# Layers 0 and 3 of a four-layer image network: a new planner with two clocks orders the instructions, layer 0 leaves the waves in two halves, and its third tile is copied by ScalarE

## The chip, the cores and the metric

The kernel runs on one core of a Trainium2 chip. The metric is device time in microseconds (us) for one execution, from a handful of runs; the profile is one further execution under the hardware profiler. TensorE (PE) multiplies matrices into PSUM; VectorE (DVE), ScalarE (ACT) and GpSimd (POOL) do elementwise work; SyncE (SP) and GpSimd issue the transfers here. [...]

## The reference

The input x is float32, 4 images x 48 channels x 256 x 256. Four layers, each of the form x = x + f(groupnorm(x)):

```
layer 0:  h = w_in (48 -> 192) . x;  h = depthwise 3x3(h);  g = gelu(h1) * h2   (96 each)
          y = w_out (96 -> 48) . g;  y = irfft2(rfft2(y in 8x8 blocks) * fft_w)
layers 1, 2:  four scans (down, up, right, left): row = x_row + conv1d(previous row)
layer 3:  y = w_in (48 -> 288) . x;  y = irfft2(rfft2(y in 8x8 blocks) * fft_mask)
          y = depthwise 3x3(y);  g = gelu(y1) * y2   (144 each);  out = w_out (144 -> 48) . g
```

## The kernel before, in words

Everything is float32. The images are worked on in two pairs. Only layers 0 and 3 matter here; the scans between them have an order of their own.

**Layer 0** (`layer0`, L150) goes through 64 strips of 8 rows of an image pair. Per strip n:

- `fetch` (L228) loads 9 rows through SP; `normed` (L237) applies the group norm on ScalarE.
- `fill(n, True)` with `hidden_rest` (L269): two pieces, each two matmul calls (L272) for the third tile of hidden channels, `rest`, copied out of PSUM by VectorE (L276). `fill(n, False)` with `hidden`: two pieces for the other 128 channels (L264), copied into `main` by ScalarE (L267). `halo` (L249) lets GpSimd carry two rows over from the strip before (L256).
- The depthwise convolution of `main` is done on TensorE by two *lanes* (`lane`, L280): each takes half the channels and, for each of two images, does nine taps as matmuls with diagonal weights (L293). A *lane round* is one tap of each lane; lane 1 starts four rounds after lane 0. When its nine taps are done, lane 0 takes gelu on ScalarE (L304), lane 1 multiplies on VectorE (L307), which frees their PSUM tiles.
- The convolution of `rest` is done on VectorE by a *unit* (`unit`, L312): a first tap on ScalarE (L322), 16 half-tile taps on VectorE (L328), gelu on ScalarE (`curve`, L336 to L338), two products (L342).
- `mixed` (L355) multiplies by w_out (L363, L370), ScalarE copies to y (L376); `turned` (L382) transposes (L387, copies L391); `waves` (L396) goes to the 64 waves (L405), VectorE applies the mask (L409); `back` (L416) returns to pixels in two rounds of a loop (64 matmul calls each way of q0, L430), VectorE adds the residual (16 instructions, L441) and takes statistics (L448); GpSimd's queue stores (L451).

All PSUM tiles of layer 0 come from one pool of four (tag "w"): the two lanes hold one each, the pieces share the others.

**Layer 3** (`layer3`, L846) goes through 33 steps of 8 rows for each of two image pairs (the last is a short tail): `normed` (L945, ScalarE L950), `turned`, `waves`, eight pieces of `spectra` (two matmul groups L996 and two masks on VectorE each, L998 and L1002), five pieces of `back` (`pixels`: L1033, copies L1042) that fill the tiles a0, a1, b0, b1, m; lanes for a and m (L1054), for the lower half of b (L1070; `lower_gate` L1077: gelu L1080, product L1081), gates L1097 with gelu L1091; VectorE units for the upper half of b (first tap L1111, taps L1114, products L1125); `store` with `mixed` (L1132: L1140, L1150, residual L1163).

**What sets the order.** [...] `in_turns` (L516) runs rounds: it advances both lanes by one tap, adds to a credit, emits the next piece from `work` while the credit is not negative and the piece's condition holds (a piece is: condition, TensorE cost, what to emit, VectorE cost), and then lets `aside` (L549) emit taps of the units for as long as a running sum `ahead` (TensorE's time spent less the pieces' VectorE costs, between -4.0 and 2.5) is above 0. What follows a unit's taps (`curve`, the products) waits for a count of calls. In layer 0 `mixed` waits for all six users of a strip (`taken`) and then for four more askings (`gone`, L484). Neither knows of ScalarE.

## Time and profile before

| what | us |
|---|---|
| median of 3 runs (lowest, highest) | 13858.08 (13811.36, 13867.86) |
| the profiled execution's own time | 13799.8 |
| its span | 13798.0 |
| TensorE busy (90% of the span) | 12409.4 |
| VectorE busy (53%) | 7347.8 |
| ScalarE busy (28%) | 3850.6 |
| GpSimd busy (10%) | 1334.0 |

Stages by the first matmuls of each in the trace: statistics of the input to 251 us; layer 0 to about 3231; the two scan layers to about 9178; layer 3 to the end.

A line of a group reads: source line, engine, operation, tile written <- tiles read, shapes, count | total busy us, mean ns | idle time of the engine just before, and what ended it. A line of the waits: engine, tile, line <- what it waited for: us in total, times, longest. In a row of stretches the granted TensorE clock (1.00 is full speed) comes after the five engines' busy times, then the share of the DMA engines that was busy and GB/s. "Issue" means that the profile shows nothing that the engine waited for. Busy matmul time is modelled at its ends, so full is not peak.

### The profile page before, as it was taken

To read this page: it belongs to the slowest core of one execution; us is meant where nothing else is said; L and a number is where in the kernel's file an instruction comes from. 1 tells how busy PE (TensorE), PEld (TensorE's weight loads), DVE (VectorE), ACT (ScalarE), POOL (GpSimd) and SP (SyncE) were. 2 spreads that over 40 slices of the span, in tenths; PEclk is the share of its full clock that TensorE was granted. 3 is DMA by queue.
4 is the path that set the end of the run, shared out by engine and by line. 5 is a ranking of instruction groups with operands and counts; after the bars stand their busy time and mean duration, and the time that the engine had idled before them with its cause. 6 is when DMAs were issued, how large, how long until landed. Compare 5 with 4: busy or idle time off the path is not lost.

```text
span 13798.0 us, 419051 instructions
## 1 busy us (share of the span) xinstructions
PE 12409.4 (90%) x195140; PEld 7360.8 (53%) x195140; DVE 7347.8 (53%) x11937; ACT 3850.6 (28%) x4710; POOL 1334.0 (10%) x977
## 2 busy tenths in 40 slices
PE   2888898888999899879998998779999999999999
PEld 1333333335777677657776776544444445444444
DVE  6777777774333334443333344455555556555555
ACT  1333333332223100002232000034443434443443
POOL 0000010000000003430000014400000000000000
PEclk9999999999999999989999999889999999999999
DMA  7222222225755876767657767711101101101100
GB/s 169 53 50 52 56 54 53 50 54 96 153 142 152 159 153 143 190 156 152 134 153 169 149 133 183 183 37 26 26 22 26 26 22 26 26 22 26 26 22 24
DMA packets 1170329, 1224.15 MB, mean 89 GB/s; under 512 B 1027668, under 2 KB 1031756, under 8 KB 1107724
## 3 DMA queue, kind: packets, MB, share of 16 engines
q1 hardware_dynamic: 1070476, 649.55, 23.6%
q0 software_dynamic: 87488, 445.55, 11.7%
q10 hardware_dynamic: 10624, 102.24, 3.7%
q8 instruction: 1532, 25.10, 0.8%
q14 instruction: 209, 1.71, 0.0%
HBM read 699.76 MB, written 497.42 MB: 87 GB/s over the span
## 4 chain that ended last, share of the span: by engine, by line
PE 78%; DMA 7%; DVE 6%; ACT 4%; issue 3%; POOL 1%; SPq 1%; ACTq 0%; DVEq 0%; POOLq 0%
PE acc L632 35%; PE pd L1054 10%; PE pd L293 9%; PE pz L996 4%; PE pd L1070 4%; PE pp L1033 4%; DMA blk<-x 3%; PE po L1150 2%; PE ph L272 2%; ACT u L950 2%; PE ph L264 2%; DMA x<-blk 2%; DMA gx<-in_x 1%; DVE acc L328 1%; POOL blk L825 1%
## 5 line engine op out<-in xcount | busy, mean ns | idle before, releaser
L632 PE MATMUL acc<-line,w_down 96*96 96x256 f32 x12240 | 2650.7, 379 | 53.1 <-DMA in<-x 31.3
L632 PEld LDWEIGHTS acc<-line,w_down 96*96 96x96 f32 x12240 | 1996.1, 163 | 707.0 <-issue 53.8
L1054 PE MATMUL pd<-z_a,diag 32*32 32x512 f32 x37152 | 1853.0, 606 | 44.9 <-issue 31.5
L293 PE MATMUL pd<-main,diag 32*32 32x512 f32 x36864 | 1522.9, 653 | 112.3 <-issue 103.9
L632 PE MATMUL acc<-line,w_left 96*96 96x256 f32 x6120 | 1358.1, 385 | 248.7 <-DVE line L815 248.7
L1114 DVE SCALAR_TENSOR_TENSOR acc<-z_b,wd,acc 128x1024 f32<-128x1024 f32 (+1 forms) x1056 | 1328.9, 1260 | 311.5 <-ACT acc L1111 279.6
L632 PE MATMUL acc<-line,w_right 96*96 96x256 f32 x6120 | 1335.2, 380 | 102.5 <-DVE line L776 38.1
L632 PEld LDWEIGHTS acc<-line,w_left 96*96 96x96 f32 x6120 | 1014.2, 166 | 592.2 <-DVE line L815 254.7
L328 DVE SCALAR_TENSOR_TENSOR acc<-rest,wd,acc 128x1024 f32<-128x1024 f32 x1024 | 1279.0, 1299 | 2.0
L632 PEld LDWEIGHTS acc<-line,w_right 96*96 96x96 f32 x6120 | 1002.1, 164 | 435.6 <-DVE line L776 40.1
L1070 PE MATMUL pd<-z_b,diag 32*32 32x512 f32 x18432 | 1065.5, 603 | 34.0 <-DVE z L1002 22.3
L293 PEld LDWEIGHTS pd<-main,diag 32*32 32x32 f32 x36864 | 534.9, 107 | 917.0 <-issue 800.6
L776 DVE SCALAR_TENSOR_TENSOR line<-acc,b_right,in 96x256 f32<-96x256 f32 x1020 | 489.2, 480 | 879.6 <-PE acc L632 835.1
L998 DVE TENSOR_TENSOR z<-pz,mask 128x512 f32<-128x512 f32 x1024 | 702.8, 686 | 458.8 <-PE pz L996 455.0
L695 DVE TENSOR_TENSOR line<-acc,in 96x256 f32<-96x256 f32 x1020 | 429.3, 421 | 944.5 <-PE acc L632 928.4
L108 ACT ACTIVATE nrm<-nrm 96x4 f32<-96x4 f32 (+2 forms) x4 | 0.8, 204 | 3323.3 <-DVE nrm L107 3323.3
L1054 PEld LDWEIGHTS pd<-z_a,diag 32*32 32x32 f32 x37152 | 593.6, 103 | 587.0 <-issue 431.1
L735 DVE SCALAR_TENSOR_TENSOR line<-acc,b_down,in 96x256 f32<-96x256 f32 x992 | 476.0, 480 | 808.7 <-PE acc L632 808.7
L1033 PEld LDWEIGHTS pp<-c_inv,z 64*64 64x64 f32 x36864 | 602.1, 136 | 463.4 <-issue 253.2
L1033 PE MATMUL pp<-c_inv,z 64*64 64x64 f32 x36864 | 672.2, 222 | 170.6 <-DVE g_b L1081 86.0
L825 POOL TENSOR_TENSOR blk<-blk,line 96x1024 f32<-96x1024 f32 x248 | 705.7, 2873 | 860.2 <-DVE line L815 444.6
L815 DVE SCALAR_TENSOR_TENSOR line<-acc,b_left,in 96x256 f32<-96x256 f32 x992 | 475.5, 479 | 525.4 <-PE acc L632 525.4
(158 smaller groups left out, 12337.0 us busy)
## 6 DMA issues: line engine op xcount, KB each, us to landing
blk<-x ACTq DMA_DIRECT2D x64, 1536.0 KB, 23.2
in<-x SPq DMA_DIRECT2D x248, 384.0 KB, 11.5
dn<-line POOLq DMA_DIRECT2D x124, 768.0 KB, 9.6
rt<-line POOLq DMA_DIRECT2D x124, 768.0 KB, 10.2
in<-rt SPq DMA_DIRECT2D x124, 768.0 KB, 7.3
in<-dn SPq DMA_DIRECT2D x120, 768.0 KB, 7.1
in<-up SPq DMA_DIRECT2D x240, 384.0 KB, 11.0
up<-blk POOLq DMA_DIRECT2D x56, 1536.0 KB, 23.9
```

The lines of the kernel that those rows point to most:

```text
L293: nc.tensor.matmul(pd[32 * j : 32 * j + 32, i], diag[s, t, :], z[s, R2 * j + t // 3 : R2 * j + t // 3 + R2, t % 3 : t % 3 + W], start=(t = ...
L328: nc.vector.scalar_tensor_tensor(to, at(t, r), wd[:, 1, t : t + 1], to, ALU.mult, ALU.add)
L632: self.nc.tensor.matmul(acc, w[:, t, :], carry[:, :, t : t + m], start=(t == 0), stop=(t == 2))
L735: nc.vector.scalar_tensor_tensor(inner(line), acc, bd, new[p][r], ALU.add, ALU.add)
L776: nc.vector.scalar_tensor_tensor(blocks(inner(line)), blocks(acc), br, new, ALU.add, ALU.add)
L825: (nc.vector if w0 == 0 else nc.gpsimd).tensor_tensor(part, part, inner(ln[p][:, f::2])[..., lo:hi].rearrange("p w i h -> p i h w"), ALU.add)
L996: nc.tensor.matmul(pz[:, b, 0 : 2 * HD], xf[s, q, :], wi[s, :], start=True, stop=True)
L998: nc.vector.tensor_tensor(z[:, q, 0 : 2 * n].rearrange("p (b c) -> p b c", b=2), pz[:, :, 0:n], mask[:, :, 0:n].to_broadcast([128, 2, n]), ...
L1033: nc.tensor.matmul(pp[to, l, q1, :], z[f, q0 + q, k * NM + 64 * c : k * NM + 64 * c + 64], self.inv1[f, :], start=True, stop=True,)
L1054: nc.tensor.matmul(pd[32 * j : 32 * j + 32, i, 0:n, :], diag[s, 2 if g == "m" else half, t, :], zt[g][s, R2 * j + t // 3 : R2 * j + t // 3 ...
L1070: nc.tensor.matmul(pd[to, i], diag[s, half, t, :], zt[f"b{half}"][s, R2 * j + t // 3 : R2 * j + t // 3 + R2, t % 3 : t % 3 + W], start=(t ...
L1114: nc.vector.scalar_tensor_tensor(made[0], at(t), wd[:, half, t : t + 1], made[0], ALU.mult, ALU.add)
```

## The change

The diff, cut to what it does. `hidden_rest` copies with ScalarE, both chunks in one instruction where they are of equal height; `back` handles one half (q0 = 0 or 8) per call and each half is a piece of its own; the planner keeps two clocks, `self.pe` and `self.dve`. Taps are emitted while `self.dve` is at most `self.pe + 1.0`; a piece with a VectorE cost is emitted only when `self.dve < self.pe + 1.5`; what follows the taps has a due time on the TensorE clock; a tile counts as free, and a strip or step as ready for `mixed`, only when the TensorE clock has passed the VectorE clock of its last use (`until`). `gone` is removed. In layer 3 the same planner is used, with clock entries for the gates and products; its computation is untouched.

```diff
@@ hidden_rest
+                if all(r1 - r0 == R2 for r0, r1 in chunks):
+                    chunks, ph = [(chunks[0][0], chunks[-1][1])], ph.rearrange("p i r w -> p (i r) w").unsqueeze(1)
                 for i, (r0, r1) in enumerate(chunks):
-                    nc.vector.tensor_copy(rests[n % 2][:, 0, r0 + 1 : r1 + 1, 1 : W + 1], ph[:, i, 0 : r1 - r0, :])
+                    nc.scalar.copy(rests[n % 2][:, 0, r0 + 1 : r1 + 1, 1 : W + 1], ph[:, i, 0 : r1 - r0, :])
@@ lane of layer 0, after the product L307
+                            self.after(self.pe + 1.0, 1.3)
+                            until[n] = max(until.get(n, 0.0), self.dve)
@@ unit of layer 0
-                last = [(3, 0.0, curve)] + [
-                    (2 - k, 1.28, lambda k=k: product(slice(64 - 64 * k, 128 - 64 * k))) for k in range(2)
+                last = [(0.3, 0.0, curve)] + [
+                    (2.2 - k, 1.28, lambda k=k: product(slice(64 - 64 * k, 128 - 64 * k))) for k in range(2)
                 ]
-                return lambda: (n, 1) in ready, start, taps, last
+                return lambda: self.pe >= full.get(n, 1e9), start, taps, done, last
@@ back
-            def back(n, z):
+            def back(n, z, q0):
...
-                for b in range(2):
+                for b in range(2 if q0 == 0 else 0):
                     nc.sync.dma_start(res[64 * b : 64 * b + C], self.x0[p, b * C : (b + 1) * C, h0 : h0 + RB, :])
...
-                for q0 in range(0, NQ, 8):
+                for q0 in (q0,):
...
+                if q0 + 8 < NQ:
+                    return
@@ work of layer 0
+                                if rest:
+                                    full[n] = self.pe + 4.0
-                        yield always, 1.8, go, 1.2 * rest
+                        yield always, 1.8, go, 0.0
...
-                            lambda: taken.get(n - 1, 0) == 6 and gone(), 4.0, lambda: state.update(y=mixed(n - 1)),
+                            lambda: taken.get(n - 1, 0) == 6 and self.pe >= until[n - 1], 4.0,
+                            lambda: state.update(y=mixed(n - 1)), 0.0,
...
-                        yield always, 2.2, lambda: back(n - 1, state["z"]), 7.0
+                        yield always, 2.0, lambda: back(n - 1, state["z"], 0), 1.7
+                        yield always, 1.1, lambda: back(n - 1, state["z"], 8), 4.4
-            self.in_turns([lane(0), lane(1)], work(), 0.52, self.aside([unit(n) for n in range(len(strips))]))
+            self.in_turns([lane(0), lane(1)], work(), 0.54, [unit(n) for n in range(len(strips))])
@@ in_turns, new
+        self.pe, self.dve = 0.0, 0.0
+        side, going = self.aside(units), True
...
+            self.pe += 0.54 * moved
             credit = min(credit + pace * moved, 2.0)
+            while piece and (credit >= 0 or not moved) and piece[0]() and (not piece[3] or self.dve < self.pe + 1.5):
                 piece[2]()
+                if piece[3]:
+                    self.after(self.pe + 1.0, piece[3])
+                self.pe += piece[1]
+                credit, moved = max(credit - piece[1], -5.0), 1
                 piece = next(pieces, None)
+            got = True
+            while got:
+                got = next(side, None)
+                going = got is not None
+            idle = 0 if moved else idle + 1
+            self.pe += 0.0 if moved else 0.3
+    def after(self, when, cost):
+        self.dve = max(self.dve, when) + cost
@@ aside, new
+        def due():
+            while later and self.pe >= later[0][0]:
+                at, cost, work = later.pop(0)
                 if cost:
+                    self.dve = max(self.dve, at) + cost
                 work()
...
+                begun[k] = self.pe + 3.0
                 units[k][1]()
...
+                while k not in begun or self.dve > self.pe + 1.0 or self.pe < begun[k]:
+                    begin(k)
+                    due()
+                    yield False
...
+                self.dve = max(self.dve, begun[k]) + cost
@@ layer 3
+                self.after(self.pe + 1.0, 1.3)                      (lower_gate; gate: 0.1 + 0.6 * k)
+                until[step] = max(until.get(step, 0.0), self.dve)
...
-                last = [(3, 0.0, curve)] if half == 0 else [(2, 1.28, product)]
+                last = [(0.3, 0.0, curve)] if half == 0 else [(0.3, 1.28, product)]
...
-                    free = lambda: last not in steps or k == 4 or taken.get((last, order[k]), 0) == units[order[k]]
+                    free = lambda: last not in steps or k == 4 or (
+                        taken.get((last, order[k]), 0) == units[order[k]]
+                        and self.pe >= until.get((last, order[k]), 0.0)
+                    )
...
-                    done = lambda: step in full and all(taken.get((step, g), 0) == units[g] for g in order)
+                    done = lambda: step in full and self.pe >= until[step] and all(
+                        taken.get((step, g), 0) == units[g] for g in order
+                    )
```

## The prediction

> **What bounds the kernel now.** I read the busy table in the page's order first (TensorE 90% of the span, VectorE 53%, ScalarE 28%), then the granted clock by stage, then TensorE's waits and its timeline in the two stages that the change touches. Layer 0 runs from 251 to 3231 us, the two scan layers to about 9178 us, layer 3 to 13770 us. The scans use neither planner and keep their time.

> A row of the stretches below: from:to, length, then busy time (and instructions) of TensorE, its weight loads, VectorE, ScalarE, GpSimd; then granted clock, DMA share and GB/s. First line: the middle of layer 0. The others: two short pieces of single strips.

> ```profile
> 600.00:2990.00 2390.00, 2115.25 (x40933) 855.80 (x40933) 1775.62 (x2359) 883.17 (x823) 226.84 (x207) 0.93 0.24 53
> ```

> ```profile
> 1500.00:1505.00 5.00, 2.12 (x40) 1.07 (x38) 5.00 (x5) 1.84 (x2) 1.53 (x1) 0.91 0.00 0
> 1505.00:1510.00 5.00, 4.62 (x66) 2.43 (x72) 5.00 (x5) 2.78 (x3) 0.00 (x0) 0.50 0.00 0
> ...
> 1545.00:1550.00 5.00, 3.03 (x72) 1.35 (x40) 5.00 (x5) 2.15 (x2) 1.53 (x1) 1.00 0.00 0
> 1550.00:1555.00 5.00, 3.71 (x57) 1.87 (x72) 5.00 (x6) 2.44 (x3) 0.00 (x0) 0.69 0.00 0
> ```

> See two losses: TensorE is idle 11% of layer 0's middle, and its clock is 0.93 there, because a piece with little TensorE work is followed by one at 0.50 or 0.69. VectorE is full in just these pieces. TensorE's own waits in that stretch (total us, times, longest):

> ```profile
> PE pt L387 <- DVE g L307: 140.0, 49, 3.3
> PE pd L293 <- issue: 91.2, 52, 4.5
> PE po L430 <- issue: 21.7, 9, 4.6
> PE pt L387 <- ACT gl L304: 12.3, 25, 0.5
> ```

> and what VectorE does ahead of that product (start, length, from the timeline):

> ```profile
> 1544.87 1.29 DVE L276 COPY rest<-ph 128x512 f32<-128x512 f32 x2 [0.51 <-PE ph L272]
> ...
> 1546.08 4.03 DVE L328 SCALAR_TENSOR_TENSOR acc<-rest,wd,acc 128x1024 f32<-128x1024 f32 x3
> ...
> 1550.02 1.21 DVE L307 TENSOR_TENSOR g<-gl,pd 128x1024 f32<-128x1024 f32 x1
> ...
> 1551.29 1.19 PE L387 MATMUL pt<-c_ident,y 112*128 112x112 f32 x8 [3.26 <-DVE g L307]
> ```

> The four PSUM tiles are all in use: the second transpose tile takes the one that lane 1 has just finished, and its product (L307) stands behind two copies (L276) and three taps (L328). So once per strip TensorE stands 3.3 us and then runs at half clock. The other large wait, "issue", has no releaser: it comes while the strip's loads run (at 1527.70 and 1571.40 the DMA share is 0.5 to 0.9), so I take it to be late instructions.

> In layer 3 (9178 to 13770 us: clock 0.99, TensorE 4303.04 of 4592 us) the waits are small:

> ```profile
> PE pp L1033 <- DVE g_b L1081: 75.4, 59, 3.0
> PE pp L1033 <- issue: 49.6, 65, 2.9
> PE pz L996 <- DVE g_a L1097: 30.0, 27, 1.1
> ```

> [...]

> **One strip of layer 0 now.** The first mixed matmuls (L363) start at 302.67, those of the last strip at 3210.81: 63 periods of 46.16 us. TensorE's work at full clock, from start to start in the timeline: 18 lane rounds, two of them in 2.28 us (1540.57 to 1542.85), 20.5; main matmuls (L264) 2 x 1.92; rest matmuls (L272) 2 x 1.91; L363 1.92; L370 1.90; transposes 2 x 0.98; L405 1.67; L430 2.0: sum 37.6 us. The stretch of 2390 us holds 51.8 strips, so the waits are 140.0/51.8 = 2.7 us (L307), 112.9/51.8 = 2.2 (issue), all others 0.4: 5.3. The rest, 46.16 - 37.6 - 5.3 = 3.3, is slow clock (a mean of 0.93 costs 3.2).

> **The change part by part.**
> 1. *Rest copy to ScalarE.* Per strip VectorE loses 4 copies, 2.58 us (two take 1.29), ScalarE gains 2 of 1.01 us. ScalarE goes from 883.17/51.8 = 17.1 to 19.1 us per strip: hidden. VectorE falls from 34.3 (1775.62/51.8) to 31.7 us, below TensorE's 37.6, so it can't be the bound. The copies leave the queue ahead of L307: 1.29 us less in that wait. Behind the new copies on ScalarE stand the first tap L322 (which needs them anyway; its 290.5 us of waiting on VectorE ends), gelu L304 and the y copies; a wait for the rest matmuls (1.9 us) now holds those up. GpSimd's halo copy then waits for ScalarE instead, which nobody needs for 10 us.
> 2. *Two clocks.* Taps are emitted while the VectorE clock is at most 1.0 us ahead of TensorE's, so at a product at most 2.3 us is queued plus its own 1.2, against 1.29 + 3.94 + 1.2 now. Prices in the plan are near the measured (tap 1.28 against 1.22 to 1.30, gate 1.3 against 1.21, VectorE's halves of back 1.7 + 4.4 against 3.26 + 2.46 in sum). The transposes still come about one lane round after the product's emission, so the wait of 2.7 us falls to between 0.1 and 1.4; I take 0.5. Bounds 0 and 2.7.
> 3. *Clock.* Without a 3.3 us hole the half clock goes; the issue waits of up to 4.5 us still cause it at times. 3.3 falls to 0.6 (bounds 0.2 and 3.3).
> 4. *Mixed waits for the clock instead of four askings.* The gate's VectorE time must have passed: 2.3 to 3.6 us after the lane ends, against 3.1 now (1528.25 to 1531.39). Behind it stand all later pieces of the strip; the fill for the next strip comes some nine lane rounds later, and lane 0 needs it 14 rounds after the strip's end. Now there are two rounds to spare; one round later means TensorE can wait for ScalarE's main copy, up to 1.1 us. Other waits go from 0.4 to 0.8 (bounds 0.2 and 3).
> 5. *Back in two halves.* Same 128 matmul records and 16 additions; each half needs one PSUM tile, not two. The residual load is issued with the first half, the store and the four statistics with the second: SP's and GpSimd's queues keep their order. If the second half and mixed follow each other, mixed's second tile waits for 1.63 us of additions; in part 4's bound.
> 6. *Issue waits* stay at 2.2: the DMAs and the instruction count are unchanged.
> Sum: 37.6 + 0.5 + 2.2 + 0.8 + 0.6 = 41.7 us, 4.46 less, x 63 = **281 us**.
> 7. *Layer 3.* 64 full steps in 4592 us, near 71 us each with the two short ones; VectorE 2651.55/4592 = 58%. Its largest wait, L1081, is late because gelu L1080 stands on ScalarE behind the eight L950 (4.0 us at 11521.71), and the plan knows no ScalarE clock: it stays. L996 behind L1097 (30.0 us) and a part of the others goes, and the earlier taps cost nothing as VectorE is idle there. I take 0.5 us per step, 32 us; bounds -1.5 and +2 us per step (-96 and +128), as a reordered step can pair its lanes better or worse and nothing in the trace shows which.
> Total 281 + 32 = 313. The profiled execution took 13799.8 us (span 13798.0 and 1.8 around it): 13487 for it. The runs' median, 13858.08, is 58 higher; taken from that, **13545 us**.

> **Rivals.**
> A, the forecast, 0.50: 13545, its own range 13430 to 13680.
> B, the waits go altogether, 0.14: layer 0 at 37.6 + 1.0 for rests, 7.56 us x 63 = 476, and layer 3 gains 1.5 us a step, 96: 13286. For it: every engine but TensorE has room. Against: the issue waits have nothing to do with order.
> C, the wait only changes its owner, 0.18: the transposes or the lanes wait for ScalarE or for the back halves instead, long enough to halve the clock; 1.5 us a strip is left, 95 us: 13763. For it: four PSUM tiles, all taken, and no ScalarE clock in the plan.
> D, the order is nearly the same, 0.06: both planners are paced by the same lane credit and mixed comes at the third round in both; then only the copy's 1.29 us moves behind other waits: 13840.
> E, slower, 0.12: in layer 3 each of the eight spectra pieces must now find VectorE's clock within 1.5 us of TensorE's, while the taps fill that clock to 1.0 and each piece adds 2.0 for 2.28 us of TensorE. If each waits one lane round more (8 x 1.08 = 8.6 us a step) and the lanes have run dry by then, 64 x 8.6 = 553 us are lost: 13858 + 553 - 281 = 14130. It decides from 281/64 = 4.4 us a step. Against: lanes normally have work, and VectorE is idle 42%.

> **How the numbers follow.** The predicted time is A's. The range 13280 to 13770 takes in A, C and B's own time and leaves out D and E (0.18). Some 0.5% (69 us) is what a measurement of this kernel tells from no change. Faster by more: A and B whole, most of C (0.80); within: D and the rest of C (0.08); slower: E (0.12).

> **What would show it.** Right: no L276 on VectorE; the wait of L387 for L307 under 50 us in the stretch 600 to 2990, granted clock there at 0.97 or more, L363 every 41 to 42.5 us, issue waits about as now; layer 3 within 130 us of 4592. Wrong: a strip of 44 us or more with a new releaser of 2 us per strip (ScalarE's copies, additions L441), or layer 3 longer by over 100 us with spectra (L996) standing apart. If the issue waits vanish, I misread them and B is near.

## The result and the profile after

| | before | after |
|---|---|---|
| median of 11 runs each, us | 13854.97 | 13781.12 |
| lowest to highest | 13811.36 to 13871.05 | 13761.88 to 13807.79 |
| span of the profiled execution | 13798.0 | 13779.3 |
| layer 0 with what comes before it, to the first scan matmul | 3270.2 | 3100.9 |
| the two scan layers | 5803.2 | 5801.6 |
| layer 3, first transpose to the end | 4724.6 | 4876.8 |

The ratio is 0.9956, with a 95% interval of 0.9944 to 0.9968: 74 us by the medians against 313 forecast, and outside the range. The stages, read from the first instruction of each in the traces, tell why the sum is so small: layer 0 became 169 us shorter, layer 3 became 152 us longer.

These two come from one execution each, and the profiled execution of the kernel before, 13799.8 us, was faster than all of its eleven runs; so they leave a gain of only 19 us. How far stages of equal code differ between profiles is seen in the runs below: layer 3 by the old planner took 4724.6, 4731.6, 4743.6 and 4747.2 us (before, e12, e1, e16), so its loss is 130 to 152 us. By the runs' times instead, e1, which has the new layer 0 and the old layer 3, gains 1.23%, some 170 us, and the kernel after gains 0.79% less than e1, so layer 3 lost some 110 us. (Layer 3 is counted here from its first transpose, 9073.4 us before, to the end; the prediction's 4592 us began at 9178 and ended at 13770.)

In layer 0 mixed (now L369) starts at 301.25 us for the first strip and at 3042.01 for the last: 43.50 us a strip, against 46.16. Its middle stretch, in the columns of the prediction's first fence:

```profile
600.00:2990.00 2390.00, 2203.56 (x43533) 886.47 (x43521) 1738.88 (x2283) 1024.70 (x982) 231.81 (x222) 0.95 0.26 56
```

TensorE is busy 92% instead of 89%, its clock 0.95 instead of 0.93. Its waits there (the four largest, and the only one left for a lane's product):

```profile
PE ph L264 <- ACT main L267: 86.7, 40, 2.2
PE pd L295 <- issue: 67.2, 36, 3.3
PE po L439 <- issue: 24.8, 16, 3.2
PE py L369 <- DVE xo L450: 2.0, 5, 0.4
...
PE pd L295 <- DVE g L309: 0.2, 1, 0.2
```

The wait for the lane's product, 140.0 us before, is gone from the transposes altogether. In its place stands a wait that was not in the list before: the fill's second matmuls (L264) want the PSUM tile of the first, and ScalarE has not yet copied it (L267). ScalarE's timeline in one strip shows what it did instead:

```profile
1502.74 2.38 ACT L326 ACTIVATE acc<-rest,none,wd 128x1024 f32<-128x1024 f32 x2
1505.14 1.05 ACT L341 ACTIVATE gr<-acc 64x1024 f32<-64x1024 f32 x1
1506.22 1.06 ACT L342 ACTIVATE gr<-acc 64x1024 f32<-64x1024 f32 x1
1507.31 1.04 ACT L343 COPY acc<-acc 64x1024 f32<-64x1024 f32 x1
1508.25 1.91 ACT L267 COPY main<-ph 128x1024 f32<-128x1024 f32 x2
```

The first taps of one unit and the curve of the one before it, 5.5 us, were emitted in one place, just ahead of the fill.

In layer 3 the largest waits of TensorE (stretch 9300 to 13550, first after, then before):

```profile
PE pp L1049 <- DVE g_b L1097: 163.1, 55, 4.1
PE pp L1049 <- issue: 78.7, 89, 2.1
```

```profile
PE pp L1033 <- DVE g_b L1081: 80.0, 61, 3.0
PE pp L1033 <- issue: 56.7, 70, 2.9
```

The same wait (g_b is what the lower gate's product writes), twice as long; and the mean clock of layer 3 fell with it, from 0.99 to 0.97. One step of each shows what TensorE waits for. ScalarE, first before, then after:

```profile
11521.71 4.04 ACT L950 ACTIVATE u<-raw,scp 112x256 f32<-112x256 f32 x8
11525.77 1.01 ACT L1080 ACTIVATE gl<-pd 64x1024 f32<-64x1024 f32 x1
```

```profile
11465.40 4.03 ACT L966 ACTIVATE u<-raw,scp 112x256 f32<-112x256 f32 x8
11469.46 1.01 ACT L1096 ACTIVATE gl<-pd 64x1024 f32<-64x1024 f32 x1
```

and TensorE, first before, then after:

```profile
11528.09 1.21 PE L1033 MATMUL pp<-c_inv,z 64*64 64x64 f32 x64 [1.97 <-DVE g_b L1081]
```

```profile
11466.55 1.18 PE L1049 MATMUL pp<-c_inv,z 64*64 64x64 f32 x64
11471.79 1.77 PE L1049 MATMUL pp<-c_inv,z 64*64 64x64 f32 x64 [4.06 <-DVE g_b L1097]
```

The second half of the back piece for b0 needs the PSUM tile of the lower gate, whose gelu stands behind normed (L966, eight instructions, 4 us): the gelu's own matmuls (L1086) end at 11465.33, and it starts at 11469.46, as normed ends. In 61 of the 64 steps of either kernel this gelu comes directly after normed on ScalarE. (Layer 0's product before is the same on VectorE: lane 1's matmuls L293 end at 1547.11, L307 starts at 1550.02, as the three taps emitted ahead of it end.) TensorE arrives at that tile 2.3 us after normed began (11467.73 less 11465.40); before, it arrived 4.4 us after (the matmuls resumed at 11528.09 after 1.97 us of waiting, so from 11526.12 on, and normed began at 11521.71). Arriving 2.1 us earlier, it waits 2.1 us longer.

The other steps show the same. Of the 64 steps with a normed, 58 have this wait before and 60 after. In both kernels TensorE goes on 6.4 us (median) after normed began, which is normed, gelu and product in a row; but it arrives 5.0 us after normed's start in the mean before, and 3.4 us after.

### The profile page after: what moved, and what is told of

Same layout as the page of the kernel before. It is cut to its first block, busy times and chain, and to the rows that moved or that the text cites. A ratio compares the mean times of both kernels' runs of the same rounds, so it can differ in the third digit from the quotient of the medians.

```text
span 13779.3 us, 418888 instructions
## 1 busy us (share of the span) xinstructions
PE 12392.8 (90%) x195140; PEld 7384.6 (54%) x195140; DVE 7174.0 (52%) x11679; ACT 3961.4 (29%) x4844; POOL 1328.2 (10%) x977
## 3 DMA queue, kind: packets, MB, share of 16 engines
q8 instruction: 1532, 25.10, 0.8%
## 4 chain that ended last, share of the span: by engine, by line
PE 78%; ACT 7%; DMA 7%; DVE 4%; issue 3%; POOL 1%; SPq 1%; ACTq 0%; DVEq 0%; POOLq 0%
PE acc L648 35%; PE pd L1070 11%; PE pd L295 8%; PE pd L1086 5%; PE pz L1012 4%; PE pp L1049 4%; DMA blk<-x 3%; PE po L1174 2%; PE ph L272 2%; ACT u L966 2%; DMA x<-blk 2%; DVE acc L1135 1%; DMA gx<-in_x 1%; PE ph L264 1%; PE py L369 1%
## 5 line engine op out<-in xcount | busy, mean ns | idle before, releaser
L1070 PE MATMUL pd<-z_a,diag 32*32 32x512 f32 x37152 | 1858.7, 616 | 41.9 <-issue 34.1
L295 PE MATMUL pd<-main,diag 32*32 32x512 f32 x36864 | 1434.6, 626 | 74.7 <-issue 70.8
L1086 PE MATMUL pd<-z_b,diag 32*32 32x512 f32 x18432 | 1049.3, 600 | 54.5 <-DVE z L1018 35.2
L1049 PE MATMUL pp<-c_inv,z 64*64 64x64 f32 x36864 | 695.4, 227 | 294.3 <-DVE g_b L1097 178.8
L1070 PEld LDWEIGHTS pd<-z_a,diag 32*32 32x32 f32 x37152 | 638.2, 104 | 589.3 <-issue 404.7
L295 PEld LDWEIGHTS pd<-main,diag 32*32 32x32 f32 x36864 | 503.1, 105 | 797.4 <-issue 684.7
L1049 PEld LDWEIGHTS pp<-c_inv,z 64*64 64x64 f32 x36864 | 625.8, 140 | 564.4 <-issue 291.4
L758 ACT COPY blk<-line 96x1024 f32<-96x1024 f32 (+2 forms) x264 | 482.1, 1890 | 935.0 <-DVE line L751 756.3
```

The source lines that it names most:

```text
L295: nc.tensor.matmul(pd[32 * j : 32 * j + 32, i], diag[s, t, :], z[s, R2 * j + t // 3 : R2 * j + t // 3 + R2, t % 3 : t % 3 + W], start=(t = ...
L758: nc.scalar.copy(blk[p][:, :, e, lo:hi, k // 2 : k // 2 + RH], inner(ln[p][:, e::2])[..., lo:hi].rearrange("p h i w -> p i w h"),)
L1049: nc.tensor.matmul(pp[to, l, q1, :], z[f, q0 + q, k * NM + 64 * c : k * NM + 64 * c + 64], self.inv1[f, :], start=True, stop=True,)
L1070: nc.tensor.matmul(pd[32 * j : 32 * j + 32, i, 0:n, :], diag[s, 2 if g == "m" else half, t, :], zt[g][s, R2 * j + t // 3 : R2 * j + t // 3 ...
L1086: nc.tensor.matmul(pd[to, i], diag[s, half, t, :], zt[f"b{half}"][s, R2 * j + t // 3 : R2 * j + t // 3 + R2, t % 3 : t % 3 + W], start=(t ...
```

## The experiments

**What was compared.** Theory A: layer 3 lost time because the new order brings TensorE to that PSUM tile earlier in relation to normed. Theory S: layer 0's gain fell short because the plan knows no ScalarE clock, so one wait took another's place. Their rivals: E of the prediction (the spectra are held back), and late instructions. All ratios are to the kernel before on the same chip. "Layer 3" below is the stage time read like that of the table. A "strip" is read from the second of mixed's two lines of matmuls, first to last over 63: 46.2 us before, 43.55 after. The kernel after and the six runs with its layer 0 gave strips of 43.2 to 43.55 us, and the seven runs that share e3's layer 3 took 4686 to 4724 us for it: smaller differences between single profiles mean nothing.

**e1: new planner in layer 0, old one in layer 3.** The layer's entries into the two clocks and its waits for them go too; only the call is shown.

```diff
-            self.in_turns([lane(0), lane(1)], work(), 0.55, [unit(s, k) for s in steps for k in range(2)])
+            side = self.aside_old([unit(s, k) for s in steps for k in range(2)])
+            self.in_turns_old([lane(0), lane(1)], work(), 0.55, side)
```

> Layer 0 by the new planner (with its other edits), layer 3 by the planner of before. Theory (the change gained in layer 0 and lost in layer 3, each by itself): layer 0 stays 169 us shorter, layer 3 returns from 4877 to about 4725 us, so about 13855 - 169 = 13686 us, ratio to before 0.988. Rival (the time comes back elsewhere because of something common to the whole run, such as the clock): layer 3 stays long, ratio 0.995.

Measured 13668.26 us, ratio 0.9877 (0.9859 to 0.9894); strip 43.4 us, layer 3 4743.6 us. Gain and loss are separate, as the theory has it: the old planner in layer 3 takes 133 us of the loss away and leaves layer 0's gain.

**e3: normed after the second back piece**, on the kernel after.

```diff
-                    if ahead:
-                        state["u"] = normed(nxt)
                     yield back(step, 2)
+                    if ahead:
+                        state["u"] = normed(nxt)
```

> The kernel after, with layer 3's eight normed activations emitted after the second back piece instead of ahead of it; the computation is the same. Theory A (TensorE waits for the lower gate's product, whose gelu stands on ScalarE behind the 4 us of normed): the wait of L1049 for the product falls from 163 us (stretch 9300 to 13550) to under 40, the half clock goes with it, layer 3 falls from 4877 to 4640-4730 us, ratio to before 0.980 to 0.986. Rival E of the prediction (spectra pieces held back until the lanes are dry): nothing changes, ratio 0.995.

Measured 13613.46 us, ratio 0.9829 (0.9814 to 0.9844). The wait is gone from TensorE's list:

```profile
PE pp L1049 <- issue: 90.1, 110, 2.8
PE pd L1070 <- issue: 46.0, 57, 2.6
PE pd L1086 <- DVE z L1018: 33.3, 61, 1.4
```

Layer 3 takes 4713.7 us, 163 less than after, with a clock of 0.99 again. Taking the stall away takes the whole loss away. It doesn't show that nothing else got worse: the 80 us that the kernel before waited for this product are gone as well, and yet the layer is only 11 us shorter than before. The issue waits of its matmuls came to 100 us before and are 150 now (same stretch).

**e5: no hold of the spectra in layer 3**, on the kernel after.

```diff
-            while piece and (credit >= 0 or not moved) and piece[0]() and (not piece[3] or self.dve < self.pe + 1.5):
+            while piece and (credit >= 0 or not moved) and piece[0]() and (not piece[3] or self.dve < self.pe + hold):
```

with hold 1.5 in layer 0 and 1e9 in layer 3.

> The kernel after, but in layer 3 pieces are not held back by the VectorE clock (the clock itself still counts them). Rival E: layer 3 returns to about 4725 us or below, ratio 0.984. Theory A: the hold only shifts the pieces by a round or two against the lanes, and so how far normed stands ahead of the lower gate's gelu; the wait of L1049 changes by up to 2 us a step in either direction, and the layer's time follows this wait (163 us now) and not the number of rounds.

Measured 13798.07 us, ratio 0.9962 (0.9947 to 0.9977); layer 3 4883.4 us, the wait 180.1 us. Rival E is refuted: it had the sign and not the mechanism. (Theory A holds no less: TensorE arrives 3.1 us after normed's start here.)

**e4: the same move of normed on the kernel before.**

> The kernel before with the same one move of normed. Theory A: the same stall was there in a smaller form (80 us and some half clock), so layer 3 falls from 4725 to about 4600-4650 us, ratio 0.991 to 0.995. Rival E: ratio 1.000.

Measured 14031.03 us, ratio 1.0130 (1.0114 to 1.0145): a miss in sign. The old stall is gone, but another stands there:

```profile
PE po L1150 <- DVE g_m L1097: 143.4, 44, 4.3
PE pp L1033 <- issue: 68.6, 92, 2.9
```

Now the m gate's gelu stands behind normed (in one step normed runs from 11466.68 for 4.04 us, and this gelu starts at 11471.75), and the old planner lets store follow at once. So moving normed helped only under the new order, which keeps store away from that gate.

**e15: e3 without layer 3's waits for the TensorE clock** (the two `self.pe >= until` conditions).

> The kernel after with normed late in layer 3 (13613 us, layer 3 in 4714), without layer 3's waits for the TensorE clock to pass the VectorE clock. With the planner of before the same move of normed made TensorE's store wait 143 us for the product of the m gate, whose gelu then stood behind normed. Theory U (the clock waits are what keeps store from being emitted ahead of that product): the wait of L1174 for L1115 appears with 100 us or more in the stretch 9300 to 13550, layer 3 takes 4830 to 4950, 13730 to 13850 us. Rival (another part of the planner avoids it): within 0.3% of 13613.

Measured 13658.61 us, ratio 0.9867 (0.9852 to 0.9882), layer 3 4752.7 us:

```profile
PE pp L1049 <- issue: 72.3, 95, 2.2
PE po L1174 <- DVE g_m L1115: 32.1, 35, 2.4
```

The wait returns with 32 us, not the 100 expected, and layer 3 is 39 us longer than in e3. The clock conditions keep store off that product in part; what else in the planner does was not found.

**e6: the kernel after without these two conditions; e17: the kernel after with layer 3's units begun without the 3.0 us delay.** Both ask which part of the planner moved TensorE's arrival.

> The kernel after, but in layer 3 the two waits for the TensorE clock to pass the VectorE clock (tile free, store ready) are left out; the rest of the planner stays. If these waits are what shifted the pieces against the lanes (theory A2), the wait of L1049 for the lower gate's product returns from 163 to about 80 us and layer 3 from 4877 to about 4740. If something else in the planner shifted them (the delayed units, the due times; theory A3), layer 3 stays at 4850 to 4900 us.

> The kernel after, but in layer 3 the plan lets a unit's taps begin at once instead of 3.0 us after its first tap was emitted. If this delay shifted the pieces: the wait of L1049 for the product falls from 163 to about 80-110 us, layer 3 from 4877 to 4740-4800. If not: 4850 to 4900, and the time within 0.3% of the kernel after.

e6: 13735.33 us, ratio 0.9924 (0.9906 to 0.9942), layer 3 4831.6 us; the wait for g_b falls to 89.3 us, but 42.9 us for g_m come up at the same matmuls. So the conditions moved most of the arrival: without them TensorE reaches this tile 4.5 us after normed's start (5.0 before, 3.4 after), and the wait for g_b is 9 us longer than before, not 83. But without them other waits come up, 25.2 us for g_a at L1086 besides those for g_m, and of layer 3's loss only 45 us come back. e17: 14044.06 us, ratio 1.0152 (1.0135 to 1.0169), layer 3 5131.7 us: neither of the two that were expected. VectorE now stands 501.3 us (244.3 in the kernel after) at a tap whose first tap ScalarE has not written (L1136 behind L1133), and TensorE's wait for g_b is 187.0 us. That the products queue behind this tap is likely and not shown: in e3 VectorE stands 428.0 us at the same place, and layer 3 is short. The delay is useful and not what moved TensorE's arrival.

**e7: rest copy back on VectorE**, on e3 (the two lines of hidden_rest undone, 1.2 us in the plan).

> The kernel after with normed late in layer 3 (13613 us, a strip of layer 0 in 43.2 us), and layer 0's rest copy back on VectorE, with its 1.2 us in the plan as before. My sum: the copy's 2.6 us on VectorE stand again ahead of the lane's product, part of the wait for it returns, 0.5 to 1.5 us a strip longer, 13645 to 13710 us. Rival (the new clocks alone cured that wait, and ScalarE is the engine now waited for): same or shorter, 13560 to 13615.

Measured 13575.02 us, ratio 0.9808 (0.9794 to 0.9823); strip 43.1 us. My sum is wrong, the rival right: undoing the copy costs nothing here (e14 below undoes it under another order of ScalarE, and there it does).

**e12: the copy alone, on the kernel before.**

> The kernel before with only layer 0's rest copy moved to ScalarE (one instruction for both chunks, no VectorE cost in the plan). My sum of the prediction: 1.29 us of the product's wait go, 13855 - 63 x 1.3 = 13770 us, and less if the half clock stays. Rival (the old planner gives the freed VectorE time to taps at once, which then stand ahead of the product): within 0.3% of before.

Measured 13789.77 us, ratio 0.9959 (0.9944 to 0.9974); strip 46.0 us by the profile, which was of the slowest of its four executions, while that of before was of a fast one. By the medians it is 54 us faster, between the sum (85 us) and the rival (at most 0.3%, 42 us). TensorE's waits in the stretch 600 to 2990:

```profile
PE pd L295 <- issue: 91.8, 47, 3.8
PE pt L389 <- ACT gl L306: 88.2, 25, 5.2
PE po L432 <- issue: 46.2, 15, 4.7
PE pt L389 <- DVE g L309: 39.0, 23, 2.7
```

Of the 140 us for the product, 39 are left, and the wait for lane 0's gelu on ScalarE at the same transposes has grown from 12 us to 88.

**e16: the two clocks alone in layer 0** (e1 with the copy on VectorE and the way back whole).

> The kernel of e1 (new planner in layer 0, old in layer 3; 13668 us, strip 43.4) with layer 0's rest copy back on VectorE and the way back in one piece, each with its cost in the plan: the two clocks alone. If they earned layer 0's gain: strip 42.8 to 43.9, 13630 to 13710 us. If two of the edits can stand in for each other but not all be left out: strip 44.5 to 46, 13740 to 13840.

Measured 13626.43 us, ratio 0.9844 (0.9830 to 0.9859), strip 43.0 us: the clocks alone earn layer 0's whole gain, and 0.33% more than e1 with all three edits. TensorE's wait for lane 1's product (L307) is 30.8 us here, 0.6 a strip; 88.7 us for lane 0's gelu (L304) have come up at the lanes.

**e9: the curve's three instructions apart**, on e3. The products after them come later in the plan, too.

```diff
-                last = [(0.3, 0.0, curve)] + [
-                    (2.2 - k, 1.28, lambda k=k: product(slice(64 - 64 * k, 128 - 64 * k))) for k in range(2)
+                last = [(w, 0.0, lambda k=k: curve(k)) for k, w in enumerate((0.3, 2.2, 2.2))] + [
+                    (1.2, 1.28, lambda k=k: product(slice(64 - 64 * k, 128 - 64 * k))) for k in range(2)
```

> The kernel after with normed late in layer 3, and the three ScalarE instructions of layer 0's curve emitted 2.2 us of the plan apart instead of in one piece; the first product comes 2.2 plus 1.2 later. Theory S (what replaced the old wait in layer 0 is TensorE's wait for the main copy L267 behind 5.5 us of curve and first taps on ScalarE, 86.7 us in the stretch 600 to 2990, and the half clock after it): that wait falls below 45 us, the strip from 43.2 to 41.8-42.6, 13530 to 13580 us. Rival (late instructions set the strip): no change within 0.3%.

Measured 13502.33 us, ratio 0.9757 (0.9742 to 0.9771), strip 42.06 us. This is the fastest kernel of the study that does the whole computation. TensorE's waits:

```profile
PE pd L295 <- issue: 64.1, 35, 3.4
PE po L441 <- issue: 47.8, 21, 4.4
PE ph L264 <- ACT main L267: 23.1, 22, 1.1
```

and ScalarE in one strip, now with the copies in between:

```profile
1506.74 1.93 ACT L267 COPY main<-ph 128x1024 f32<-128x1024 f32 x2 [0.58 <-PE ph L264]
1508.69 1.05 ACT L341 ACTIVATE gr<-acc 64x1024 f32<-64x1024 f32 x1
1509.78 1.93 ACT L267 COPY main<-ph 128x1024 f32<-128x1024 f32 x2
1511.59 1.06 ACT L343 ACTIVATE gr<-acc 64x1024 f32<-64x1024 f32 x1
```

Theory S holds: with the burst on ScalarE spread, the wait for L267 falls from 89.0 us (e3) to 23.1, and the strip from 43.2 us by 1.2.

**e10: layer 0's units may begin 10 instead of 4 us after the rest fill**, on e3.

> The kernel after with normed late in layer 3, and layer 0's units may begin 10 instead of 4 us of the plan after the rest tile's last matmul, so that the first taps (2.4 us on ScalarE) come after the fill's copies. Theory S: the wait of L264 for L267 falls below 45 us, strip 41.8 to 42.8, 13530 to 13595 us. Rival: VectorE starts its taps too late and mixed waits for the unit, 13620 or more; or no change (late instructions).

Measured 13661.65 us, ratio 0.9870 (0.9855 to 0.9885), strip 44.1 us. The fill's wait for L267 is down to 1.1 us as the theory said, but lanes waiting 148.2 us for lane 0's gelu (L306) stand in its place: the burst on ScalarE was moved, not spread.

**e8: the way back in one piece; e14: the rest copy on VectorE**, both on e9.

> The kernel e9 (normed late, curve apart; 13502 us, strip 42.1), with layer 0's way back emitted in one piece again (3.1 us on TensorE, 6.1 on VectorE in the plan). If the halves matter (two PSUM tiles at once make the next lane or mixed wait for the additions L450), waits for L450 of 1 to 2 us a strip appear and the time is 13565 to 13630. If the two clocks alone made layer 0 faster, it stays at 13480 to 13530.

> The kernel e9 with the rest copy back on VectorE as well, two ScalarE microseconds a strip fewer ahead of the fill's copies. Theory S: what is left of the waits for ScalarE (35 us in the stretch) goes, the strip falls to 41.3-41.9, 13450 to 13495 us. Rival (VectorE at 34.3 of 42 us a strip becomes late for the products): 13510 to 13560.

e8: 13516.18 us, ratio 0.9761 (0.9747 to 0.9776), strip 42.04 us: the halves make no difference. e14: 13574.61 us, ratio 0.9804 (0.9790 to 0.9819), strip 42.65 us, a miss: the transforms L411 now wait 45.2 us for lane 0's gelu and 14.5 us for the product. So the copy is worth having on ScalarE (0.47%) once the curve is spread there, while with the curve in one piece it cost 0.2 to 0.3% (e7 against e3, e16 against e1; e16 also has the way back whole).

**e13: e9 without layer 0's loads.**

> The kernel e9, with layer 0's strips from the third on computed from stale rows: their two loads (the rows and the residual, 0.77 MB a strip) are left out, the store stays. Theory I (the issue waits of layer 0 are instructions that come late because the bulk loads occupy the DMA engines): the issue waits fall from 112 us in the stretch 600 to 2990 to under 50, the strip from 42.1 to 40.3-41.3, 13390 to 13460 us. Rival (they have to do with the instruction count alone, or with the store): waits stay at 90 or more and the time within 0.3%.

Measured 13327.76 us, ratio 0.9626 (0.9610 to 0.9642). Layer 0 ends at 2813 us here, so the stretch to compare is 600 to 2750, first e9, then e13:

```profile
600.00:2750.00 2150.00, 2000.01 (x40347) 823.89 (x40329) 1608.35 (x2114) 954.18 (x919) 217.39 (x203) 0.97 0.27 57
```

```profile
600.00:2750.00 2150.00, 2100.53 (x44228) 887.69 (x44226) 1754.13 (x2331) 1024.44 (x989) 243.83 (x223) 1.00 0.12 23
```

The issue waits there fall from 112 to 2.6 us, and the strip from 42.06 to 38.94. The issue waits are indeed tied to the loads. (What was left out is more than the expectation says: the rows and the residual are 0.8 MB a strip each, 1.5 to 1.6 MB together.)

The DMA records of the kernel after point to instructions that come late: 51 of its 53 issue waits of over 0.3 us (TensorE, 600 to 2990) end 1.2 to 1.6 us after a block of the instruction queue (1532 packets of 16.4 KB in the run) landed; of the 46 other waits 5 do. Whether and how the loads delay these blocks is not shown: a block takes about as long to move without them (1.06 us in e13 against 1.12 in the kernel after, in the median).

## Why the prediction was wrong, by its own steps

**1. Rest copy to ScalarE.** It was to take 1.29 us out of the product's wait, for copies of 1.01 us on ScalarE (L267, of the same shape, took 1012 ns in the mean before; the new copy L278 takes 1013). Done alone (e12) it took 2 us a strip out, and gave 1.5 of them to a wait for ScalarE; undoing it cost nothing while the curve stood in one piece on ScalarE (e7), and some 65 us once it was spread (e14). "Hidden" looked at ScalarE's total (17.1 to 19.1 us a strip), not at what stands in its queue at the moment when a PSUM tile must come free.

**2. Two clocks.** The wait for the product fell from 2.7 us a strip to none together with the copy, and to 0.6 by the clocks alone (e16), against 0.5 taken. This step was right, and e16 shows that it alone made the strip faster.

**3. Clock.** Taken at 0.6 us a strip, measured 0.05 of the clock over a strip of 43.5, 2.2 us. Of layer 0's terms this is the most mis-sized. It assumed that only waits of 3.3 us and more bring the half clock. That was the author's estimate, from waits of 3.3 us with pieces at a clock of 0.50 or 0.69 behind them; such a limit is not shown, and the last section has what the traces show.

**4. Other waits.** Taken at 0.8 us, measured (86.7 + 2.0 + 1.6 and a few of 1 us or less)/54.9 = 1.7 us a strip. The place was named (ScalarE's main copy), but for another reason: not the fill coming late for a lane, but first taps and curve in one burst on ScalarE.

**5. Halves.** Expected without effect of their own; e8 agrees.

**6. Issue waits.** Taken at 2.2 us, measured 1.8; right, and the DMA records point to the cause it named, late instructions. Their full price was missed: with the half clock that follows them, the loads cost 3.1 us a strip (e13 against e9).

With the measured terms the sum is 37.6 + 0 + 1.8 + 1.7 + 2.2 = 43.3, against 43.50 measured: the frame held. Steps 3 and 4 were 2.5 us a strip too small, steps 2 and 6 gave 0.9 of that back, and 0.2 stay open. So layer 0 gained some 170 instead of 281 us, between A and C. That the whole came out within 18 us of C's 13763 is luck: C has 95 us gained in layer 0 and nothing in layer 3, and not a larger gain and a loss that takes most of it back.

**7. Layer 3** is the step that failed. It was forecast 32 us faster, with a bound of 96 us on the slow side, and lost 152 by the profiles, some 110 by the runs' times. "It stays" was said of the wait behind normed, with the right reason (ScalarE's order is not in the plan). But a wait behind a fixed piece lasts as long as TensorE arrives ahead of that piece's end, and the change moves arrivals: 2.1 us in the step shown, 1.6 us in the mean. The wait for the product grew from 80 to 163 us, and what the half clock took in layer 3 (half of the time spent at it) from 63 to 136 us. The prediction treated the length of that wait as a constant, and put the half clock after it at nothing. e3 shows that without this wait no loss is left. What moved the arrival is in the main the two clock conditions (e6: the wait is back at 89 us without them); the hold (e5) and the units' delay (e17) are out. Why leaving the conditions out gives only 45 us back, with new waits for g_m and g_a in the place of the old, is not settled.

## What to carry to other kernels

When an order changes, a wait for an engine that the plan leaves out does not stay as it was (here it went from 80 to 163 us): write down when the waiting engine arrives relative to the piece that blocks it, and price one round of shift either way. A plan with clocks for two engines can leave the bursts to the third (here 5.5 us on ScalarE, and 86.7 us of waits behind it); a sum of busy times per stage doesn't show that, the third engine's timeline around each PSUM release does. And price a stall together with the half clock after it: in layer 3, 83 us more of this wait came with 73 us more lost at half clock.

## What was not expected of the hardware

Loads with a low mean rate (e9 moves 57 GB/s in all from 600 to 2750 us, with the DMA engines busy 27% of it) still cost TensorE time: without 1.5 MB of loads a strip (e13) the issue waits went from 112 to 2.6 us in 2150, and the clock from 0.97 to 1.00, while the store stayed.
